# Layer 1's routing: the last three strips settled beside the first expert tiles, the first plan made later, the rows waiting on the sends themselves

## The chip, the cores and the metric

The kernel runs on one core of one Trainium2 chip. The metric is the device time of one launch in microseconds (us); the median of several runs is compared. A profiled execution has its own time, and a span from its first to its last recorded instruction.

## The reference

A two-layer "metaformer" on x of shape (2, 256, 56, 56). Each layer mixes in space (layer 0: attention in a window of 7; layer 1: two ternary 3x3 convolutions with batch norm), adds that to x, and then runs a mixture of experts over the 6272 tokens. Cut to what the change touches (layer 1's experts):

```
t = tokens of x                      # 6272 x 256
u = layer norm of t
logits = u @ gate_w + gate_b         # 8 experts
cw = the two largest of softmax(logits), zero elsewhere
out = sum over e of cw[:, e] * (gelu(u @ W1[e] + b1[e]) @ W2[e] + b2[e])   # hidden 512
t = t + out
```

All of it is float32.

## The kernel before

The experts are not run over all tokens. Each token is sent to its two experts, so that the expert matmuls run over sorted rows.

**Strips.** The tokens lie in 14 strips (7 of 8 image rows for each of two images). A strip has 3 groups of 128 tokens when its number is even and 4 when it is odd. `strip(i)` is a generator with five steps: (1) load the residual `back` (SP), add the convolution's result (DVE L2208, ACT L2211), transpose to token layout (PE `pt`, L2221); (2) add `back` (DVE L2225) and take statistics; (3) scale into `u` (ACT L762); (4) transpose `u` (PE `pu`, L810) and multiply with the gate (PE `pl`, L822); (5) write the logits `lgs` (DVE L831).

**Settling.** `settle(strips)` takes a batch of strips and gives each of their tokens its two experts and its two places in the DRAM table `xs`, which has a region for each expert. It is a generator too: best expert (DVE), second expert (DVE), ranks within the expert (PE `rk`, L892 to L895, with DVE `hots` ahead), places (DVE L904 to L908); then one step for each group, which issues two indirect DMAs from POOL (L929) that scatter the group's rows into `xs`. The batches are strips 0 to 4 one by one, then 5-6, 7-8, 9-10, 11-12 and 13.

**Early and late.** Strips 0 to 8 are early (`FIRST[1]` is 9): their 31 groups are sent while strips are worked on. After strip 8 has been settled, enough rows are known to fill 23 full tiles of 256 rows (`EARLY[1]`). `tiles(0)` plans these: a matmul counts the rows by expert (PE `counts`, L985), some 20 DVE operations find for each tile its expert and its first row (`where`). The sends of strips 9 to 13 are held back (`held`) and go out beside the tiles.

**The loop.** `all_strips()` runs 16 iterations. In iteration i, strip i does its step 1, strip i-1 its steps 2 to 4, and strip i-2 its last step; when strip i-2 ends a batch, the first three steps of its `settle` follow, and the fourth comes in the next iteration. In iteration 11, once strip 8's sends have been issued, the first plan is made and `fence()` issues a small DMA on POOL that reads `xs`. In iteration 13 `next(experts1)` has SP load the weights of tiles 0 to 2 (L1140, 1154 KB each; the expert's number is read from `where`). After the loop the second plan is begun, SP reads what the fence brought (`value_load(fences[0])`, L2328), and the expert stage starts.

**The expert stage.** SP fetches the rows `xg` of tiles 0 to 4 (L1129, 260 KB each; there are 41 full tiles and 23 half tiles in all). For each tile PE transposes the rows (`pt`, L1150), multiplies with W1 (`ph`, L1182) and W2 (`py`, L1201); ACT applies GELU, DVE adds the bias (`y`, L1211), POOL scatters the result into `ys` (L1213). Rows are fetched 4 tiles ahead and weights 3. Four times in each tile `beside1` takes a step of `rest()`: in each tile one held group is sent, and two steps are done on the plans of the remaining tiles. `rest()` is brought to its end at tile 18 at the latest, since the rows of tile 23 are fetched at tile 19.

**Order.** SP, DVE, PE and ACT take their instructions in program order (`manual_schedule(engines=ENGINES)`); POOL is not among them. The fetch of an early tile's rows is declared free of dependences on all sends (`rows1`); the fence stands in for them. PSUM: the strips use a pool of their own (`route_ps`) that is closed before the tiles' pool (`pt` 2, `ph` 4, `py` 2 banks) is opened.

The lines after the last tile gather each token's two results and write the output.

Of the kernel before, what the change touches and what calls it, by code (L numbers as in the profile page):

```python
# [2 lines left out]

# [1 line left out]

# [639 lines left out]
def metaformer(ctx: ExitStack, tc: tile.TileContext, a: dict, out: bass.AP, flag):  # L645
# [5 lines left out]
    class Banks:  # L651

        def __init__(self, pool, wide=False):
            self.pool, self.wide = pool, wide

        def tile(self, *args, **kw):
            return self.pool.tile(*args, **kw)

    def disjoint(inst, group, others):

        inst = inst.ins
        tc.declare_no_dep(inst, group=others, reason="rows apart")
        tc.add_to_no_dep_group(group, inst)
# [432 lines left out]
    def experts_in_order(layer, FF, plans, ys, wp, at_tile):  # L1096
# [25 lines left out]
        def fetch_rows(j):  # L1122
            where, _, _, n = planned(j)
            r = nc.sync.value_load(
                where[0:1, 1, n : n + 1], min_val=0, max_val=E * ROWS - G
            )
            gp = blocks_of(j)
            xg = tp.tile([P, GP, RW], F32, tag="xg", name="xg", bufs=6)
            o = nc.sync.dma_start(  # L1129
                xg[:, :gp], xs[bass.ds(r, gp * P), :].rearrange("(p i) c -> p i c", i=gp)  # L1130
            )
            if tiles[j][0] == 0:
                disjoint(o, f"early{layer}", f"rows{layer}" if layer else f"late{layer}")
            live.setdefault(j, {})["xg"] = xg

        def fetch_weights(j):
# [702 lines left out]
    with mid:  # L1839
# [338 lines left out]
        with ExitStack() as both:  # L2178
            wp1 = both.enter_context(
                tc.tile_pool(name="moe_w1", bufs=4, side="right", reuse_waits="tile")  # L2180
            )
            wp = both.enter_context(
                tc.tile_pool(name="route_w1", bufs=1, side="right", reuse_waits="tile")
            )
            tp = both.enter_context(
                tc.tile_pool(name="route_t1", bufs=2, side="right", reuse_waits="tile")
            )
            route_ps = ExitStack()
            ps = Banks(
                route_ps.enter_context(  # L2190
                    tc.tile_pool(name="route_ps1", bufs=2, space=PSUM, reuse_waits="tile")
                ),
                True,
            )

            nr = wp.tile([P, KC, RING], F32, tag="nr", name="nr")

            def residual(i):

                b, s = STRIPS[i]  # L2200
                r = X[b, s]
                ng = groups_of(i)[1]
                cols = ring(i)
                back = tp.tile([P, NTT, C], F32, tag="back", name="back", bufs=1)[:, :ng]
                nc.sync.dma_start(back, by_token(x_mid, i))
                for o in range(KC):
                    ro = r[:, o, :].rearrange("p (h w) -> p h w", w=W)
                    nc.vector.scalar_tensor_tensor(  # L2208
                        ro, ro, scale2[:, o : o + 1], inner(b, s)[:, :, o], ALU.mult, ALU.add
                    )  # L2210
                    nc.scalar.activation(  # L2211
                        in_blocks(nr[:, o, cols]),
                        narrow(ro),
                        AF.Relu,
                        bias=shift2[:, o : o + 1],
                    )
                pt = ps.tile([P, NTT, C], F32, tag="pt", name="pt")[:, :ng]
                for t in range(ng):
                    at = in_ring(i, t)
                    for k in range(KC):  # L2220
                        nc.tensor.transpose(  # L2221
                            pt[:, t, k * P : (k + 1) * P], nr[:, k, at], ident
                        )
                yield
                nc.vector.tensor_tensor(XT[b, s], pt, back, ALU.add)  # L2225

            def strip(i):
                yield from residual(i)
                yield from norm(i, XT[STRIPS[i]])

            norm, settle, tiles, planning, gates, wgt1, _, sent = routing(1, wp, tp, ps)

            def fence():

                some = wp.tile([1, 1], I32, tag="some", name="some")
                nc.gpsimd.dma_start(some, xs[0:1, 0:1].bitcast(I32))
                fences.append(some)

            def send(steps, i):

                if i >= FIRST[1]:
                    if next(steps, steps) is not steps:
                        held.append(steps)
                else:
                    finish(steps)

            def all_strips():

                n = len(STRIPS)
                jobs = {}  # L2250
                ready = iter(())
                for i in range(n + 2):
                    young, old = i - 1, i - 2
                    if young in jobs:
                        next(jobs[young])
                    send(ready, old - 1)
                    if not plans1 and FIRST[1] - 1 in sent:
                        plan, n_early = tiles(0)
                        plans1.append(plan)
                        fence()  # L2260
                    if young == 0:
                        next(jobs[young])
                    if i < n:
                        jobs[i] = strip(i)
                        next(jobs[i])
                        if i == n - 1:

                            next(experts1)
                    if young > 0 and young in jobs:
                        next(jobs[young])  # L2270
                    steps = iter(())
                    if old in jobs:
                        finish(jobs.pop(old))
                        for q in BATCHES:
                            if q[-1] == old:
                                steps = settle(q)
                    for _ in range(3):
                        next(steps, None)
                    if old == 0:
                        finish(steps)  # L2280
                    if young in jobs:
                        next(jobs[young])
                    ready = steps
                send(ready, n - 1)
                return n_early

            def last_plans():

                plan, n_full = yield from planning(1, n_early, True)
                plans1.append(plan)  # L2290
                yield
                plans1.append((yield from planning(2, n_full, True)))

            def rest():

                yield
                sending = chain(*held)
                while True:
                    more = next(sending, sending) is not sending
                    yield  # L2300
                    for _ in range(2):
                        more |= next(planned, planned) is not planned
                        yield
                    if not more:
                        return
                    yield

            plans1, fences, held = [], [], []
            gating = gates()

            def beside1(j, part):
                nonlocal route
                if route is None:
                    if part == 3:
                        next(gating, None)
                    return
                more = next(route, route) is not route
                if not more or part == 3 and j == EARLY[1] - ROWS_AHEAD - 1:
                    finish(route)
                    route = None  # L2320

            experts1 = experts_in_order(1, 2 * C, plans1, ys[1], wp1, beside1)
            route = rest()
            with tc.manual_schedule(engines=ENGINES):
                n_early = all_strips()
                planned = last_plans()
                next(planned)
                nc.sync.value_load(fences[0])  # L2328

                route_ps.close()  # L2330
                for b in range(B):
                    pads[b].close()
                tp1 = both.enter_context(tc.tile_pool(name="moe_t1", bufs=2, reuse_waits="tile"))
                ps1 = Banks(
                    both.enter_context(
                        tc.tile_pool(name="moe_ps1", bufs=2, space=PSUM, reuse_waits="tile")
                    ),
                    True,
                )
                experts1.send((tp1, ps1))  # L2340

    with ExitStack() as st:
# [164 lines left out]
```

## Time and profile before

| | us |
|---|---|
| median of 5 runs | 1715.0 (1711.0 to 1722.8) |
| profiled execution, its own time | 1719.84 |
| its span | 1718.0 |
| layer 1's routing, about 1125 to 1263 | 138 |
| expert tiles, about 1263 to 1645 | 382 |
| gathering and output, from about 1645 | 73 |

Over the span, PE is busy 1502.1 us (87%), DVE 960.1 (56%), ACT 694.6 (40%) and POOL 636.2 (37%). Times in the views are from the span's start. PE is TensorE's matmuls, PEld its weight loads, SPq the DMA issues of SP. In a line of the timeline stand the start, the duration, engine, line and operation, the tile written and those read, the shapes, the count, and in brackets how long the engine had been idle and what ended that. The matmuls' ends are modelled, and a releaser is inferred.

### The profile page before, as it was taken

Reading aid. Unit: us, or ns where it says so; the run is one execution under the profiler, and the core shown is the slowest. Engines: PE = TensorE matmul, PEld = TensorE weight load, DVE = VectorE, ACT = ScalarE, POOL = GpSimd, SP = SyncE. Lnnn points to the kernel's source line nnn. Section 1 sums busy time; section 2 is a strip of 40 time slices with the busy share of each in tenths; the row PEclk is TensorE's granted clock in tenths of the full one; section 3 lists DMA queues with packets and bytes.
Section 4 is the critical chain, followed back from the end, with each engine's and each line's share of the span. In section 5 each row is a group of like instructions: output and inputs, shape, how many; then the busy total and the mean of one; then the engine's idle time right before and its main releaser. Section 6 shows DMA issues by size and latency. Waiting matters only on the chain. (4 is left out here: it accounts for less than half of the span.)

```text
span 1718.0 us, 25578 instructions
## 1 busy us (share of the span) xinstructions
PE 1502.1 (87%) x8445; PEld 1176.8 (69%) x8445; DVE 960.1 (56%) x2620; ACT 694.6 (40%) x1419; POOL 636.2 (37%) x729
## 2 busy tenths in 40 slices
PE   5999999999878979894989879957679999999964
PEld 3556565556566867783778778746578888898852
DVE  3456667466645445976998888677743111111136
ACT  2545443453433434543444262244433334343323
POOL 2112335244343773551333323427725542222210
PEclk9999999899888999996999989955579999999975
DMA  7123334121256877984431000024457777888858
GB/s 231 56 64 91 109 98 154 34 88 62 75 170 238 286 255 292 310 302 182 173 144 71 1 1 0 10 65 143 156 186 268 272 258 266 284 288 295 297 195 322
DMA packets 94189, 291.78 MB, mean 170 GB/s; under 512 B 20183, under 2 KB 35643, under 8 KB 84960
## 3 DMA queue, kind: packets, MB, share of 16 engines
q1 hardware_dynamic: 70384, 231.82, 40.5%
q0 software_dynamic: 19856, 51.82, 7.9%
q10 hardware_dynamic: 3808, 6.42, 1.0%
q8 instruction: 69, 1.13, 0.3%
q14 instruction: 72, 0.59, 0.1%
HBM read 218.55 MB, written 74.20 MB: 170 GB/s over the span
## 5 line engine op out<-in xcount | busy, mean ns | idle before, releaser
L1182 PE MATMUL ph<-ut,w 128*128 128x256 f32 (+1 forms) x1472 | 309.5, 361 | 12.7 <-DMA w<-in_L_experts 10.8
L1211 DVE TENSOR_TENSOR y<-py,w 128x512 f32<-128x512 f32 (+1 forms) x120 | 76.8, 640 | 407.0 <-PE py L1201 387.3
L1201 PE MATMUL py<-w,h 128*128 128x256 f32 x1288 | 299.2, 381 | 2.2 <-DVE y L1211 2.2
L1182 PEld LDWEIGHTS ph<-ut,w 128*128 128x128 f32 x1472 | 250.9, 195 | 41.5 <-DMA w<-in_L_experts 12.3
L1201 PEld LDWEIGHTS py<-w,h 128*128 128x128 f32 x1288 | 244.7, 191 | 35.5 <-DVE y L1211 2.6
L929 POOL DMA_INDIRECT xs<-u,pos x196 | 194.7, 993 | 112.8 <-issue 36.3
L1213 POOL DMA_INDIRECT ys<-y,dest x136 | 136.2, 1002 | 218.0 <-DVE dest L1157 95.5
L1189 ACT ACTIVATE h<-ph,w 128x256 f32<-128x256 f32 (+1 forms) x368 | 162.8, 448 | 111.5 <-PE ph L1182 105.9
L1592 ACT ACTIVATE ex<-sc 112x476 f32<-112x476 f32 (+3 forms) x224 | 116.8, 573 | 178.0 <-PE sc L1582 176.7
L1154 ACT COPY ut<-pt 128x512 f32<-128x512 f32 (+1 forms) x120 | 65.2, 543 | 272.4 <-PE pt L1150 272.3
L1923 PE MATMUL pc<-lo,wq 128*128 128x448 f32 x336 | 133.8, 400 | 5.7 <-DVE lo L1898 5.4
L1923 PE MATMUL pc<-hi,wq 128*128 128x448 f32 x336 | 132.5, 396 | 2.4 <-DVE x L1945 1.9
L1612 DVE TENSOR_TENSOR acc<-av,acc 128x238 f32<-128x238 f32 (+3 forms) x224 | 88.3, 407 | 72.8 <-PE av L1602 72.0
L1213 POOL DMA_INDIRECT ys<-y,to x81 | 81.7, 1009 | 121.8 <-DVE dest L1157 63.5
L1602 PE MATMUL av<-ex,vals 112*64 112x238 f32 (+3 forms) x896 | 123.8, 399 | 2.8 <-DVE acc L1612 2.8
L2066 PE MATMUL pc<-hi,wq 128*128 128x448 f32 (+1 forms) x288 | 102.9, 367 | 17.8 <-ACT hi L2033 9.4
L1573 PE MATMUL sc<-q_im,keys 32*112 32x238 f32 (+3 forms) x896 | 100.3, 428 | 7.5 <-ACT ex L1592 7.4
L2066 PE MATMUL pc<-lo,wq 128*128 128x448 f32 (+1 forms) x288 | 102.1, 364 | 0.2 <-DVE lo L2034 0.2
L1896 POOL TENSOR_TENSOR v<-pad 128x928 f32<-128x928 f32 (+1 forms) x28 | 56.9, 2042 | 105.0 <-ACT pad L1879 61.0
L1602 PEld LDWEIGHTS av<-ex,vals 112*64 112x64 f32 x896 | 56.5, 141 | 51.8 <-issue 28.3
L1150 PE MATMUL pt<-ident,xg 128*128 128x128 f32 x434 | 70.3, 283 | 17.4 <-DMA xg<-xs 13.7
L1573 PEld LDWEIGHTS sc<-q_im,keys 32*112 32x112 f32 x896 | 46.3, 176 | 48.8 <-ACT ex L1592 24.1
(279 smaller groups left out, 2484.6 us busy)
## 6 DMA issues: line engine op xcount, KB each, us to landing
w<-in_L_experts SPq DMA_DIRECT2D x64, 1154.0 KB
w<-in_L_experts SPq DMA_DIRECT2D x56, 641.0 KB
xg<-xs SPq DMA_DIRECT2D x97, 260.0 KB
acc<-in_fresh SPq DMA_DIRECT2D x14, 896.0 KB
got<-ys SPq DMA_DIRECT2D x21, 512.0 KB
got<-ys SPq DMA_DIRECT2D x7, 1024.0 KB
xt<-in_x_tok SPq DMA_DIRECT2D x14, 448.0 KB
rec<-shares SPq DMA_DIRECT2D x28, 224.0 KB
```

Of the source, the lines that this page charges most:

```text
L929: w = nc.gpsimd.indirect_dma_start(xs[:, :], bass.IndirectOffsetOnAxis(ap=pos[:, j, t0 + t : t0 + t + 1], axis=0), at_of[t][0][:, at_of[t] ...
L1182: nc.tensor.matmul(ph[:, :g], w1[:, k, f * P : (f + 1) * P], d["ut"][:, k, :g], start=k == 0, stop=k == KC - 1,)
L1189: nc.scalar.activation(d["h"][:, f, :g], ph[:, :g], AF.Gelu, bias=b1[:, f : f + 1])
L1201: nc.tensor.matmul(py[:, i, :], d["h"][:, f, i * P : (i + 1) * P], w2[:, f, :], start=f == 0, stop=f == NF - 1,)
L1211: nc.vector.tensor_tensor(y[:, :gp], py[:, :gp], bcast(b2, 1, [P, gp, C]), ALU.add)
L1213: o = nc.gpsimd.indirect_dma_start(ys[:, :], bass.IndirectOffsetOnAxis(ap=d["to"][:, i : i + 1], axis=0), y[:, i, :], None, bounds_check=T ...
L1573: nc.tensor.matmul(sc[h // 2][:, h % 2, :nq], keys[g][p, c, tx * TT : (tx + 1) * TT], q_im[p, c, r0:r1, c0:c1], start=True, stop=False,)
L1592: nc.scalar.activation(e[:, :, :nq], sc[j][:, :, :nq], AF.Exp, scale=HD**-0.5)
L1602: nc.tensor.matmul(av[VW * i : VW * (i + 1), :nq], vals[g % 3][:, tx, 2 * c + j, 2 * i : 2 * i + 2, :].rearrange("p a d -> p (a d)"), ex[j ...
L1612: added = nc.vector.tensor_tensor(d, av[:, :nq].rearrange("p (h w) -> p h w", w=c1 - c0), d, ALU.add)
L1923: nc.tensor.matmul(pc[:, :NT], wq[:, k, c, dx * C + o * P : dx * C + (o + 1) * P], part[:, :, k, dx : dx + W], start=m == 0, stop=m == 2 * ...
L2066: nc.tensor.matmul(pc[:, : 2 * ns * W], wq[:, k, c, dx * C + o * P : dx * C + (o + 1) * P], part[:, : 2 * ns, k, dx : dx + W], start=m == ...
```

## The change

1. The first plan `tiles(0)` and `next(experts1)` (the weights of tiles 0 to 2) move from iterations 11 and 13 to iteration 14. Strip 13's fourth step (`pu`, `pl`) is moved ahead of them in that iteration.
2. The last two batches (strips 11-12 and 13) are no longer settled in the loop. `settling()` does their four steps beside the tiles, ahead of the later plans; `sends()` takes up their sends when it gets to them.
3. The fence is gone. The fetch of an early tile's rows is declared free of the held sends alone (`late1`), and so waits for the early sends themselves.
4. The strips' PSUM pool is closed by the time the moved steps run, so `Banks` has a lender: their tiles (`rk`, `counts`) are then taken from the rotation of `py`.

```
     class Banks:
         def __init__(self, pool, wide=False):
-            self.pool, self.wide = pool, wide
-
-        def tile(self, *args, **kw):
-            return self.pool.tile(*args, **kw)
+            self.pool, self.wide, self.lender = pool, wide, None
+
+        def tile(self, shape, dt, **kw):
+            if self.lender is None:
+                return self.pool.tile(shape, dt, **kw)
+            t = self.lender.tile([P, G // P, C], dt, tag="py", name=kw["name"])
+            t = t.rearrange("p a b -> p (a b)")[: shape[0], : int(np.prod(shape[1:]))]
+            if len(shape) == 3:
+                t = t.rearrange("p (a b) -> p a b", b=shape[2])
+            return t
...
             if tiles[j][0] == 0:
-                disjoint(o, f"early{layer}", f"rows{layer}" if layer else f"late{layer}")
+                disjoint(o, f"early{layer}", f"late{layer}")
...
-            def fence():
-
-                some = wp.tile([1, 1], I32, tag="some", name="some")
-                nc.gpsimd.dma_start(some, xs[0:1, 0:1].bitcast(I32))
-                fences.append(some)
...
                     send(ready, old - 1)
-                    if not plans1 and FIRST[1] - 1 in sent:
-                        plan, n_early = tiles(0)
-                        plans1.append(plan)
-                        fence()
                     if young == 0:
                         next(jobs[young])
                     if i < n:
                         jobs[i] = strip(i)
                         next(jobs[i])
-                        if i == n - 1:
-
-                            next(experts1)
                     if young > 0 and young in jobs:
+                        next(jobs[young])
+                    if i == n:
                         next(jobs[young])
                     steps = iter(())
                     if old in jobs:
                         finish(jobs.pop(old))
-                        for q in BATCHES:
+                        for q in BATCHES[:-2]:
                             if q[-1] == old:
                                 steps = settle(q)
+                    if i == n:
+                        plan, n_early = tiles(0)
+                        plans1.append(plan)
+                        next(experts1)
                     for _ in range(3):
                         next(steps, None)
                     if old == 0:
                         finish(steps)
-                    if young in jobs:
+                    if young in jobs and i < n:
                         next(jobs[young])
                     ready = steps
...
+            def settling():
+
+                for q in BATCHES[-2:]:
+                    steps = settle(q)
+                    for _ in range(4):
+                        next(steps)
+                        yield
+                    held.append(steps)
+                yield from last_plans()
+
+            def sends():
+
+                at = 0
+                while at < len(held):
+                    yield from held[at]
+                    at += 1
...
-                sending = chain(*held)
+                sending, others = sends(), settling()
                 while True:
                     more = next(sending, sending) is not sending
                     yield
                     for _ in range(2):
-                        more |= next(planned, planned) is not planned
+                        more |= next(others, others) is not others
                         yield
...
                 n_early = all_strips()
-                planned = last_plans()
-                next(planned)
-                nc.sync.value_load(fences[0])
-
                 route_ps.close()
...
+                ps.lender = ps1
                 experts1.send((tp1, ps1))
```

More of the change, by code (lines that the diff above doesn't have):

```diff
@@ L1 @@
 from contextlib import ExitStack, nullcontext
-from itertools import chain
 import numpy as np
@@ L2306, in rest @@
                     yield
-            plans1, fences, held = [], [], []
+            plans1, held = [], []
             gating = gates()
```

## Prediction

> **What bounds the kernel now.** I read the slices of the page first, to find the stage of the change; then the busy time by stage; then the timeline of that stage, the chain of waits in it, the waits of SP's queue, and the DMA traffic in short windows.
>
> The busy time by stage (us, then busy us and count of PE, PEld, DVE, ACT, POOL, then granted clock, DMA share, GB/s):
>
> ```profile
> 1125.00:1263.00 138.00, 90.69 (x452) 77.44 (x452) 100.81 (x420) 60.52 (x119) 74.63 (x154) 0.56 0.43 143
> 1263.00:1645.00 382.00, 381.40 (x2036) 339.69 (x2037) 68.77 (x255) 144.96 (x321) 134.18 (x136) 0.99 0.77 267
> ```
>
> The first row is the routing of layer 1's 14 strips: no engine is full, PE is at half clock, and the end is set by a chain that hops between DVE, PE and ACT. The second row is the 64 expert tiles: PE is busy 381.4 of 382 us, so a tile stage that starts x us later ends x us later, and PE work put into it is paid in full. The change touches only the seam. The timeline there:
>
> ```profile
> 1219.84 0.17 PE L985 MATMUL counts<-seen_b,all_w 128*128 128x8 bf16 x1
> 1220.06 0.17 DVE L987 COPY counts<-counts 128x8 f32<-128x8 f32 x1 [2.95 <-PE counts L985]
> ...
> 1223.88 0.17 DVE L1054 CAST where<-first 1x23 int32<-1x23 f32 x1
> ...
> 1226.14 2.35 PE L2221 MATMUL pt<-ident,nr 128*128 128x128 f32 x8 [6.13 <-ACT nr L2211]
> ...
> 1239.34 2.97 SPq L1140 DMA_DIRECT2D w<-in_L_experts  x3
> ...
> 1240.43 0.96 POOL L929 DMA_INDIRECT xs<-u,pos  x1 [0.30 <-issue]
> ...
> 1249.19 0.61 POOL L2236 DMA_DIRECT2D some<-xs  x1 [7.80 <-DMA xs<-u,pos]
> ...
> 1254.79 4.78 SPq L1129 DMA_DIRECT2D xg<-xs  x5
> ...
> 1255.97 3.16 PE L822 MATMUL pl<-gate,ut 128*128 128x8 f32 x14 [0.26 <-ACT ut L813]
> ...
> 1259.16 0.19 DVE L831 TENSOR_TENSOR lgs<-pl,gate_b 128x32 f32<-128x32 f32 x1 [4.81 <-PE pl L822]
> ...
> 1263.36 1.95 PE L1150 MATMUL pt<-ident,xg 128*128 128x128 f32 x8
> ```
>
> To be seen: the first plan (counts to where) holds DVE up in mid strips, and PE then sits idle 6.13 us ahead of strip 11's transposes. The weights of tiles 0 to 2 leave SP at 1239.34 and drain beside the last strips. The fence lets the rows go at 1254.79, and PE ends the gate products (pl) of strip 13 at 1259.13. The last settle runs on DVE from 1259.16, and PE, which takes its instructions in order, starts tile 0 (pt, L1150) at 1263.36. Weights and rows are there by then: what ends last is the settle.
>
> **The change part by part**, against this execution (span 1718.0, its own time 1719.84 us; the median of the five runs is 1715.0, 4.8 lower, and I move the sum over to it unchanged).
>
> *The first plan leaves iteration 11.* Strips 7 to 9 are 16.70 us apart (transposes at 1185.97 and 1202.67), 9 to 11 are 23.47. The excess, 6.8, and the idle time on PE, 6.1, bound the gain; I take 6.5. The chain of waits puts POOL's sends in here, since DVE's write into u (L803) follows a landing; but that gap is 0.17 to 0.27 us with a landing ahead of it and without one, and the buffer belongs to strip 3, whose sends were issued by 1188.42. So I don't let the sends bind.
>
> *The settle of strips 11 and 12 leaves the strips.* Strip 13's scaling ended at 1251.61, its transposes (L810) began at 1253.35, behind the settle's matmuls: 1.5 us less. Together PE ends pl of strip 13 at 1259.1 - 6.5 - 1.5 = 1251.1.
>
> *The plan is made in iteration 14, behind that.* In program order the counts matmul stands after pl of strip 13. Counts to the end of the second cast took 1219.84 to 1224.05, 4.2 us: 1255.3. SP loads the expert's number and issues: 1238.6 to 1239.34, 0.75 us. So the weights start at 1256.1, where before they started at 1239.34, 24 us ahead of the first tile. Queued behind that wait on SP are two more weights (1.32 apart) and the rows of tiles 0 to 4, the first at 1259.8. Nobody else waits for SP there.
>
> *Weights and rows through the DMA queue.* This is the term that decides. Three weights are 3 x 1154 KB = 3.55 MB. Alone on the queue they moved 0.85 MB in 2 us, at the slowest 0.68:
>
> ```profile
> DMA packets 103, 0.85 MB, mean 425 GB/s; under 512 B 11, under 2 KB 11, under 8 KB 11
> ...
> DMA packets 75, 0.68 MB, mean 338 GB/s; under 512 B 1, under 2 KB 1, under 8 KB 2
> DMA packets 177, 0.60 MB, mean 299 GB/s; under 512 B 27, under 2 KB 27, under 8 KB 137
> ```
>
> (windows 1248:1250, 1262:1264, 1264:1266.) So 8.4 to 10.5 us, after about 0.95 from issue to first traffic (rows issued at 1254.79, traffic from 1255.75): the third weight is in at 1265.4 to 1267.5. The last two windows say where rows issued behind a weight stand: the rows of tile 5 went out at 1261.47, 1.1 us after a weight, and while that weight drained (1262 to 1264) only 2 of 75 packets were small; the rows' small packets came after it. So tile 0's 260 KB follow all three weights: 0.6 us at 425 GB/s, 1.2 at the 218 of window 1258:1260, and 0.3 to land. pt of tile 0 starts at 1266.3 to 1269.0; I take 1267.4, or 4.0 us later than 1263.36.
>
> The Trainium skill says the same in general and thereby speaks against this change (DMA: Bandwidth & Descriptors, section "Queues, rings and completion order"): each DMA engine consumes one issuer's ring in order and round-robins only between issuers. The rows share SP's ring with the weights.
>
> *Work put into the tiles.* The matmuls of two settles (0.31 us from 1236.86 to 1237.17, about 0.3 for strip 13) and the second counts (0.19) now stand between products: +0.8 on a full PE. Waits there I cost at nothing. A step's DVE operations take about 1.3 us and PE reaches the matmul a half tile and more later (half a tile is 3.5 us); uncovered, 1.3 for each of three. A borrowed py buffer makes the next py wait for the y add just before (0.69 us), under 3.46 us of ph; uncovered, 0.9 each. DVE is busy 69 of 382 us there. The 18 held groups of sends still leave POOL one per tile (to tile 17); the later plans, 2 steps per tile, end near tile 12 instead of 8, ahead of their use at tile 19, so seven tiles of 7.35 us cover them.
>
> *The clock.* PE is now idle some 16 us before tile 0 instead of 4. Before, the clock was full 3.8 us after pt began (0.50 to 1267, 0.87 in 1267:1268). At layer 0's first tile, after a longer idle time, PE began at about 496.7 and stood at 0.50 until 502 and 0.83 in 502:504, some 5.9 us. Two us more at half clock lose 1: 0 to 1.1, I take 0.5. The Trainium skill (TensorE: Matmul & The Clock Gate, Part 1) has one idle window of about 3.4 us make PE cold, so that both waits would be equally cold; by it this term would be 0 and the sum 4.8.
>
> *The fence goes.* Costed at nothing: before, xg(0) was in hand before PE needed it, and afterwards the last early send (issued by 1241.4, 2.5 to 4.3 us to land) is in 14 us before the rows can be issued at 1259.8. The send is not what the rows hang on; the plan and SP's queue are.
>
> Sum: 4.0 + 0.8 + 0.5 = +5.3 us: 1725.1 in this execution, 1720.3 on the median. That is 0.3%; 0.5% (8.6 us) is about what a measurement of this kernel can tell from no change. The ends: +2.9 + 0.6 + 0 and +5.6 + 0.9 + 1.1, so 1718.5 to 1722.6 for this case alone, and some 3 us either way for the medians (the runs lie from 1711.0 to 1722.8).
>
> **The rivals.**
> 1. Rows do not queue behind weights. Then xg(0) lands 2.7 us after its issue, 1262.5, with the first weight (about 5 us after 1256.1, by the one issued at 1260.34) already in; tile 0 starts 0.9 earlier, and 1.3 is given back: 1715.4. Against it stand the two windows above. Chance 0.07, no change.
> 2. Slower by over 0.5%: the weights take as long as they did. From 1239.34 it was 1254 until the queue had emptied (5 packets of it still ran in 1252:1254), 14.6 us, beside 0.5 MB of other loads and some sends. Were that the weights' own pace, a few slow DMA engines for instance, xg(0) would be in at 1256.1 + 14.6 + 1.2 = 1271.9: +8.5 + 1.3, or 1724.8. It decides once pt of tile 0 starts after 1270.7 (1263.4 + 8.6 - 1.3). If the sends do bind the strips after all, the 6.5 is lost and the place is the same: 1726.8. Only 3.3 us of rows in the queue separate it from the forecast, so: chance 0.36 with both.
> 3. The parts pay: plan and settle off the strips' path are worth 8.0, the last settle's idle time 4.2. To be faster by 8.6, tile 0 must start by 1253.5, before the plan itself (1255.3) can be had. It would take counts that don't stand behind pl of strip 13: about 1705. Chance 0.07.
>
> **How the numbers follow.** The forecast has 0.50 and rival 1 0.07, together 0.57 within 0.5%; slower 0.36, faster 0.07. The range reaches down past rival 1 by 3 us of the medians, to 1712, and up past rival 2 by as much, to 1730.
>
> **What would show it.** Right: strip 11's transposes follow pl of strip 9 without the 6 us; pl of strip 13 ends near 1251; weights leave SP near 1256; SP no longer waits for sends; PE's longest idle time is about 16 us and ends with a DMA (xg), near 1267; then 7.35 us per tile as before. Wrong: rows landing before the third weight, pt of tile 0 before 1263 or after 1271, or PE waits inside tiles 1 to 5.

## The result, and the profile after

The kernel after takes 1722.0 us, the kernel before 1717.3 in the same comparison (medians of 52 and 94 runs); the ratio is 1.0027, with a 95% interval of 1.0019 to 1.0036, or 3.3 to 6.2 us slower (0.27%). The forecast was +5.3 us, and no change beyond 0.5%. The profiled execution has a span of 1719.4 us and a time of its own of 1721.13.

The two profiled executions reach the strips at different times, for reasons that lie ahead of the change: the first residual transposes (`pt<-ident,nr`) start at 1125.99 us before and at 1124.11 after. The last product of the tiles ends 4.7 us later from that start; the spans differ by 1.4 us only because 1.9 us ahead of the strips and 1.5 us behind the tiles, where nothing was changed, went the other way. So in what follows places are given from that start ("S+"), and lines as the profile has them.

The busy time by stage (us, then busy us and count of PE, PEld, DVE, ACT, POOL, then granted clock, DMA share, GB/s):

```profile
1125.00:1263.00 138.00, 89.70 (x438) 76.32 (x436) 93.09 (x378) 59.24 (x117) 74.18 (x153) 0.56 0.38 130
1263.00:1645.00 382.00, 379.46 (x2036) 337.50 (x2037) 75.25 (x293) 144.83 (x321) 133.79 (x136) 0.99 0.79 271
```

DVE has handed 6 to 8 us of settling from the first stage to the second, where it is idle most of the time. The timeline of the seam:

```profile
1217.99 1.95 PE L2226 MATMUL pt<-ident,nr 128*128 128x128 f32 x8
...
1238.81 0.96 POOL L934 DMA_INDIRECT xs<-u,pos  x1 [0.30 <-issue]
...
1241.08 2.07 ACT L767 ACTIVATE u<-x,t_nmr,t_rstd 128x256 f32<-128x256 f32 x4 [0.49 <-DMA xs<-u,pos]
1241.27 0.17 DVE L808 COPY u<-ids 128x4 f32<-128x4 f32 x1 [0.27 <-DMA xs<-u,pos]
...
1241.74 2.80 PE L815 MATMUL pu<-ident,u 128*128 128x128 f32 x8 [1.50 <-ACT u L767]
...
1245.21 3.16 PE L827 MATMUL pl<-gate,ut 128*128 128x8 f32 x14 [0.26 <-ACT ut L818]
...
1248.22 0.17 PE L990 MATMUL counts<-seen_b,all_w 128*128 128x8 bf16 x1
1248.44 0.17 DVE L992 COPY counts<-counts 128x8 f32<-128x8 f32 x1 [6.92 <-PE counts L990]
...
1252.25 0.17 DVE L1059 CAST where<-first 1x23 int32<-1x23 f32 x1
...
1252.81 2.94 SPq L1145 DMA_DIRECT2D w<-in_L_experts  x3
...
1256.67 4.79 SPq L1134 DMA_DIRECT2D xg<-xs  x5
...
1264.77 1.97 PE L1155 MATMUL pt<-ident,xg 128*128 128x128 f32 x8 [16.38 <-DMA xg<-xs]
```

Strip 11's transposes (first line) no longer wait. The gate products of strip 13 (L827) end near 1248.4, S+124.3, where before it was S+133.1. And then PE stands idle for 16.38 us, released by a DMA, the rows of tile 0. They are the last to come, behind plan, three weights and SP's queue. What SP waited for in that stretch (us in total, times, longest):

```profile
SPq L1143 <- DVE first L1058: 22.1, 1, 22.1
```

That is the load of tile 0's expert number, which waits for the plan. There is no row for the sends: when the rows were issued, the last early send had landed 15 us before (at 1241.25 by its semaphore, 2.4 us after its issue at 1238.81).

The order of weights and rows on the DMA engines can be read from the packets in windows of 2 us (1256:1258, 1260:1262, 1262:1264 and 1264:1266; weights have packets of 9232 bytes, rows of 2080):

```profile
DMA packets 103, 0.80 MB, mean 402 GB/s; under 512 B 16, under 2 KB 16, under 8 KB 16
...
DMA packets 101, 0.80 MB, mean 402 GB/s; under 512 B 14, under 2 KB 14, under 8 KB 14
...
DMA packets 221, 0.77 MB, mean 386 GB/s; under 512 B 25, under 2 KB 25, under 8 KB 170
...
DMA packets 437, 0.81 MB, mean 405 GB/s; under 512 B 48, under 2 KB 48, under 8 KB 437
```

Rows were issued from 1256.67 on, but up to 1262 the windows have not one packet between 2 and 8 KB: only the weights' large ones and tiny ones. From 1264 on no large packet is left. The three weights were in at 1264.0, 11.2 us after the first was issued, and tile 0's rows 0.7 us after that.

### The profile page after: what moved, and what is told of

The parts are those of the page before. It is cut to its first block, busy times and chain, and to the rows that moved or that the text cites. A ratio compares the mean times of both kernels' runs of the same rounds, so it can differ in the third digit from the quotient of the medians.

```text
span 1719.4 us, 25573 instructions
## 1 busy us (share of the span) xinstructions
PE 1502.4 (87%) x8445; PEld 1175.8 (68%) x8445; DVE 958.8 (56%) x2620; ACT 693.9 (40%) x1419; POOL 636.1 (37%) x728
## 5 line engine op out<-in xcount | busy, mean ns | idle before, releaser
L1607 PE MATMUL av<-ex,vals 112*64 112x238 f32 (+3 forms) x896 | 125.3, 403 | 3.3 <-DVE acc L1617 3.3
L1218 POOL DMA_INDIRECT ys<-y,to x81 | 81.6, 1008 | 124.3 <-DVE dest L1162 63.5
L1155 PEld LDWEIGHTS pt<-ident,xg 128*128 128x128 f32 x434 | 55.8, 146 | 48.1 <-DMA xg<-xs 24.5
```

The lines of the kernel that those rows point to most:

```text
L1155: nc.tensor.transpose(pt[:, k, i * P : (i + 1) * P], d["xg"][:, i, k * P : (k + 1) * P], ident)
L1218: o = nc.gpsimd.indirect_dma_start(ys[:, :], bass.IndirectOffsetOnAxis(ap=d["to"][:, i : i + 1], axis=0), y[:, i, :], None, bounds_check=T ...
L1607: nc.tensor.matmul(av[VW * i : VW * (i + 1), :nq], vals[g % 3][:, tx, 2 * c + j, 2 * i : 2 * i + 2, :].rearrange("p a d -> p (a d)"), ex[j ...
```

## The experiments

The eight kernels below the kernel after were each timed against the kernel before on the same chip, in five rounds. The places below are from each one's trace, in us from the start of the strips' first transposes; "tile 8" is the first W2 product of the ninth tile, a point at which the seam and the first settles are over.

| kernel | plan ready | first weight out | first rows out | strip 13's pl ends | tile 0 starts | tile 8 | ratio to before (95%) |
|---|---|---|---|---|---|---|---|
| before | 98.1 | 113.3 | 128.8 | 133.1 | 137.4 | 206.4 | 1 |
| after | 128.3 | 128.7 | 132.6 | 124.3 | 140.7 | 210.4 | 1.0027 (1.0019 to 1.0036) |
| later_plan_alone | 131.5 | 131.9 | 135.8 | 127.5 | 144.2 | 213.3 | 1.0037 (1.0012 to 1.0062) |
| no_fence | 98.1 | 113.8 | 121.9 | 133.4 | 137.7 | 206.6 | 0.9997 (0.9981 to 1.0012) |
| plan_where_it_was | 98.1 | 113.8 | 122.9 | 131.1 | 131.0 | 200.2 | 0.9975 (0.9959 to 0.9992) |
| rows_first | 128.3 | 128.7 | 130.0 | 124.3 | 135.1 | 205.9 | 0.9995 (0.9976 to 1.0014) |
| plan_ahead | 121.3 | 121.7 | 125.5 | 124.2 | 134.0 | 203.7 | 0.9986 (0.9965 to 1.0007) |
| plan_ahead_rows_first | 121.3 | 121.7 | 122.9 | 124.2 | 128.6 | 199.3 | 0.9935 (0.9913 to 0.9957) |
| plan_in_steps | 111.0 | 111.4 | 121.4 | 125.0 | 125.3 | 195.9 | 0.9950 (0.9924 to 0.9975) |
| plan_in_steps_rows_first | 111.3 | 111.7 | 119.4 | 125.4 | 125.2 | 195.7 | 0.9941 (0.9916 to 0.9966) |

The times agree with the places, with one exception: divided by 1717, the shift at tile 8 is +0.23% for the kernel after, -0.36% for plan_where_it_was and -0.62% for the last, inside their intervals, as are all others but plan_ahead_rows_first. That one is 7.1 us (0.42%) earlier at tile 8, while its interval begins at 0.43% and its middle is 0.65%; where the other 4 us would come from no run shows. Matmul ends are modelled, so tile 0 can "start" 0.15 us ahead of pl's end.

**The parts by themselves.** First the later plan without the rest, in the kernel before:

```
-                    if not plans1 and FIRST[1] - 1 in sent:
-                        plan, n_early = tiles(0)
-                        plans1.append(plan)
-                        fence()
...
-                        if i == n - 1:
-
-                            next(experts1)
...
                     if young in jobs:
                         next(jobs[young])
+                    if i == n:
+                        plan, n_early = tiles(0)
+                        plans1.append(plan)
+                        fence()
+                        next(experts1)
                     ready = steps
```

> The kernel before, with one edit: the first plan, the fence and the three weights are made in iteration 14, behind the gate products of strip 13; all settles stay in the strips. Theory A (the late plan is the loss): the strips gain the 6.5 us of the plan, but the weights leave SP near 131 us after the strips' first transposes (before: 113.3), the rows land behind them near 143, and tile 0 starts 5 to 6 us later than in the kernel before (137.4); the time is 5 to 6 us above the kernel before, a little more than in the kernel after, which also has the settles out of the way (1.5 us). Rival D (moved settles and py buffers are the loss): with the settles left in place the time is at or below the kernel before.

Measured: weights out at S+131.9, tile 0 at S+144.2, 6.9 us later than before; the time 0.37% up. Theory A holds, and the loss is about 1 us more than it expected (5 to 6 us): the strips gained 5.7 us in place of 6.5. PE's timeline shows both waits that follow one another there:

```profile
1269.10 0.18 PE L892 MATMUL rk<-hots,before_w 128*128 128x32 bf16 x1 [8.29 <-DVE hots L882]
...
1277.57 1.97 PE L1150 MATMUL pt<-ident,xg 128*128 128x128 f32 x8 [7.10 <-DMA xg<-xs]
```

The settle of strip 13 still stands in the strips, but it is over 7 us before the rows are in. Set against the kernel after, which differs from it in the moved settles and the fence, the settles are worth 2.9 us at tile 8 (213.3 to 210.4): they are a gain. (That the fence is worth nothing is the next run.)

Then the fence alone, in the kernel before:

```
-                disjoint(o, f"early{layer}", f"rows{layer}" if layer else f"late{layer}")
+                disjoint(o, f"early{layer}", f"late{layer}")
...
-                        fence()
...
-                nc.sync.value_load(fences[0])
```

> The kernel before, with one edit: the fence and its load are gone, and the rows of early tiles wait on the early sends themselves, as in the kernel after. Theory A (the fence was hidden, the last settle ends last): rows leave SP some 5 us earlier (the last send lands near 1249, the fence at 1254), tile 0 starts at the same place behind the settle, no change in time (within 1 us). Rival: the fence was on the path, and the time falls by 3 us or more, or the wait on many sends costs SP time, and it rises.

Measured: rows out 6.9 us earlier, tile 0 no earlier, time unchanged. The fence was hidden behind the last settle; in the timeline PE still waits for that (`hots`) and not for rows:

```profile
1267.67 0.21 PE L892 MATMUL rk<-hots,before_w 128*128 128x32 bf16 x1 [2.98 <-DVE hots L882]
...
1268.93 1.95 PE L1150 MATMUL pt<-ident,xg 128*128 128x128 f32 x8
```

Then all of the change but the later plan:

```
                     send(ready, old - 1)
+                    if not plans1 and FIRST[1] - 1 in sent:
+                        plan, n_early = tiles(0)
+                        plans1.append(plan)
...
                         next(jobs[i])
+                        if i == n - 1:
+                            next(experts1)
...
-                    if i == n:
-                        plan, n_early = tiles(0)
-                        plans1.append(plan)
-                        next(experts1)
```

> The kernel after, with the plan put back to iteration 11 and the weights back to iteration 13, as in the kernel before; the settles stay beside the tiles and the rows wait on the early sends. Theory A (the loss is the late plan alone, the moved settles are a gain): strips end some 6.5 us later than in the kernel after, but weights are in long before, so tile 0 follows the gate products of strip 13 within 1 us: about 6 us earlier than in the kernel before, less 0.6 given back in the tiles, so 5 us below the kernel before (0.3%). Rival D (the moved settles cost): tile 0 starts earlier and the time is still not below the kernel before. Rival B (the wait on the sends costs more than the fence): the rows leave SP later than 1254.8 on the clock of the kernel before, PE is idle for over 4 us, and nothing is won.

Measured: tile 0 follows strip 13 without a gap, 6.4 us earlier than before, and the time is 0.25% down:

```profile
1253.96 3.16 PE L827 MATMUL pl<-gate,ut 128*128 128x8 f32 x14 [0.26 <-ACT ut L818]
1256.98 1.95 PE L1155 MATMUL pt<-ident,xg 128*128 128x128 f32 x8
```

So the moved settles and the wait on the sends, which the change has in common with this kernel, are good for 6.2 us at tile 8 when the weights are early; in the kernel after, the later plan turns them into +4.0. Here the rows do hang on the last early send, as SP's waits show:

```profile
SPq L1134 <- DMA xs<-u,pos: 5.2, 1, 5.2
```

**The path of the kernel after.** Two edits cut it at two places. One lets rows out ahead of the second and third weight:

```
         for j in range(AHEAD):
             live[j] = {}
-            fetch_weights(j)
+            if not layer or j == 0:
+                fetch_weights(j)
         tp, ps = yield
         for j in range(ROWS_AHEAD):
             fetch_rows(j)
+            if layer and 0 < j < AHEAD:
+                fetch_weights(j)
```

> The kernel after, with one edit: in layer 1 SP issues the weights of tile 0, then the rows of tiles 0 and 1, then the weights of tile 1, rows 2, weights 2, rows 3 (before: three weights, then the rows). Theory A (the rows queue behind three weights in SP's ring): with the plan where it is, tile 0's rows follow one weight instead of three; that weight landed 5 us after its issue, so tile 0 starts some 6 us earlier than in the kernel after (16.4 us of idle time on PE become about 10), and the time falls by about 6: some 1.5 us below the kernel before. Rival B (the rows are held by the wait on the early sends, or DMA engines do not keep the order): the start of tile 0 moves by less than 1.5 us and the time stays about 4.7 above the kernel before. Rival C (the weights themselves are the wait, the rows would be in anyway): tile 0 starts earlier but tile 1 then waits for its weights, and the gain is below 3 us.

Measured: the plan and the first weight go out as in the kernel after; the rows go out only 2.6 us earlier, but tile 0 starts 5.6 us earlier, and the time falls from 1.0027 to 0.9995. The rows were held by the two weights ahead of them: 2.6 us in SP's issues, the other 3.0 us on the DMA engines. Rival B falls with that, and rival C too: PE has no other wait in the first tiles, and at tile 8 the gain is still 4.5 us (the last section says where 1.1 us went).

```profile
1262.00 2.24 PE L1155 MATMUL pt<-ident,xg 128*128 128x128 f32 x8 [10.78 <-DMA xg<-xs]
```

The other makes the plan while PE is at strip 13's gate products:

```
-                    if i == n:
-                        next(jobs[young])
                     steps = iter(())
...
                         next(experts1)
+                        next(jobs[young])
```

> The kernel after, with one edit: in iteration 14 the first plan and the three weights stand ahead of strip 13's fourth step (pu, pl) instead of behind it. DVE is idle there for 6.9 us in the kernel after. Theory A (the late plan delays weights, and rows stand behind them): the plan runs beside pu and pl, the weights leave SP 6 to 7 us earlier, tile 0 starts 6 to 7 us earlier, and the time is about 2 us below the kernel before. Rival B (the early sends hold the rows): the last of them lands near 1241 in the kernel after, so B expects no move unless that landing is later than the plan; the time stays 4.7 above. Rival D (the settle steps and the borrowed py buffers beside the tiles cost the time): the start of tile 0 moves, but at least 4 us are still lost inside tiles 0 to 5.

Measured: plan, weights and tile 0 all 6.7 to 7.0 us earlier, strip 13 no later: DVE had been idle. At tile 8 it is 2.7 us below the kernel before; the timed ratio, 0.9986, has 1 in its interval and agrees.

```profile
1263.82 1.97 PE L1155 MATMUL pt<-ident,xg 128*128 128x128 f32 x8 [9.79 <-DMA xg<-xs]
```

**Versions that beat both.** The two edits together:

> The kernel after, with both edits: the plan stands ahead of strip 13's fourth step, and SP issues weights 0, rows 0 and 1, weights 1, rows 2, weights 2, rows 3. Theory A: the two delays add up, since each is a part of the same path (plan, weights, rows): the weights leave near 121.7 us after the strips' first transposes, tile 0 starts 6.4 us after that, near 128, 9 us earlier than in the kernel before (137.4), of which about 2 are given back within the first tiles (0.6 for the settles, 1 for tile 1's weights); the time is 7 us (0.4%) below the kernel before. Rival: the edits overlap, and the time is not below that of the better one alone (2 to 3 us below the kernel before).

Measured: tile 0 at S+128.6, tile 8 at 7.1 us below the kernel before, ratio 0.9935. Tile 0 is 12.1 us earlier than in the kernel after, against 5.6 and 6.7 for the two edits alone. They add up, so plan, weights and rows are indeed one path. PE still waits 4 us for it. So the plan was spread over the places where DVE waits for PE, and the weights were put back to iteration 13:

```
                     young, old = i - 1, i - 2
+                    if i == FIRST[1] + 3:
+                        for _ in range(4):
+                            next(early)
...
                     steps = iter(())
+                    if i == FIRST[1] + 2:
+                        next(early)
+                    if i == n - 1:
+                        plan, n_early = finish(early)
+                        plans1.append(plan)
+                        next(experts1)
                     if old in jobs:
...
-                    if i == n:
-                        plan, n_early = tiles(0)
-                        plans1.append(plan)
-                        next(experts1)
                     for _ in range(3):
                         next(steps, None)
+                    if i == FIRST[1] + 1:
+                        early = planning(0)
+                        next(early)
```

> The kernel after, with the first plan taken in steps in the places where DVE waits for PE (its counts in iteration 10 behind the settle of strips 7 and 8, the rest in iterations 11, 12 and 13), and the weights in iteration 13 again. Theory A: the plan costs the strips at most 2 us instead of 6.5, weights are in before the strips end, the rows leave when the last early send has landed (near 122, beside the weights), and tile 0 starts near 126, 11 us earlier than in the kernel before: the time is 10 us (0.6%) below it. Rival (DVE has no room in the strips, so that the plan costs its 4.7 us wherever it stands): the strips end near 129 and the gain is that of the plan put back to iteration 11, about 5 us.

Measured: the plan costs the strips 0.8 us (S+124.3 to 125.0) in place of 6.5, tile 0 waits 0.3 us for its rows, and tile 8 is 10.5 us below the kernel before; timed 0.9950:

```profile
1248.84 3.16 PE L827 MATMUL pl<-gate,ut 128*128 128x8 f32 x14 [0.26 <-ACT ut L818]
1252.30 1.97 PE L1155 MATMUL pt<-ident,xg 128*128 128x128 f32 x8 [0.29 <-DMA xg<-xs]
```

Last, the same with rows first:

> As plan_in_steps, and SP issues the weights of tile 0, then rows 0 and 1, weights 1, rows 2, weights 2, rows 3. Theory A: with one weight instead of three beside the last early sends, these land near 117 to 119 instead of 122.5, rows are in before PE has ended the gate products of strip 13, and tile 0 starts with their end, near 124.5 to 125.5: 0 to 1.5 us less than plan_in_steps. Rival: the weights of tiles 1 and 2, now issued behind the rows, which wait for the sends, come too late for those tiles, and the time is above that of plan_in_steps.

Measured: the rows go out at S+119.4 instead of 121.4, since only one weight drains beside the last sends, but tile 0 can't start before strip 13 has ended: 125.2, no more than 0.2 us gained at tile 8, nor do the later weights come too late. Ratio 0.9941; the two can't be told apart. With either, PE goes from the strips to the tiles with next to no gap (0.3 us and none), so what is left to win ahead of tile 0 lies in the strips themselves.

## Why the prediction was right, point by point

*What bounds.* Right: the end of the seam is set by what PE waits for last, once the settle and now the rows, and a later tile stage costs its delay in full: +3.3 us at tile 0, +4.0 at tile 8, +4.0 at tile 19, +4.7 at the last product. The last 0.7 us come after tile 23, far behind the seam; about half of them are short waits of PE for a weight there (0.6 us in the kernel after, 0.3 before), which differ from trace to trace.

*The strips.* 8.0 us were expected, 8.9 came. The plan's removal gave 6.3 to 6.6 (strip 11's transposes at S+93.9 for 100.1, strip 13's at S+111.2 for 117.7), as sized. The settle of strips 11 and 12 gave 2.3 where I had 1.5: I let PE start strip 13's transposes after the whole scaling, but in the kernel after they start 0.66 us after it begins (L815 at 1241.74, scaling from 1241.08) and follow it group by group. The sends did not bind the strips: where the view names one (1241.27), the gap is 0.27 us, and it was 0.27 at the same place in the kernel before (1249.73), where no landing ended it.

*Plan and SP.* 4.20 us from counts to the second cast, as before. From there to the issue it was 0.39 us instead of 0.75, where SP had been standing at the load.

*Weights and rows.* The term that decided: 11.3 us expected from the first weight's issue to tile 0, 12.0 measured (0.7 more). The order was the forecast's, and rows_first shows it to be the cause. In the Trainium skill (DMA: Bandwidth & Descriptors, "Queues, rings and completion order") descriptors are consumed in ring order on each engine; the windows above and the 5.6 us of rows_first agree. Rival 1 is out with that. Rival 2 is out too: with nothing else beside them the weights took 11.2 us, not 14.6, and the third landed within 0.8 us on all engines.

*Work in the tiles.* +0.8 expected; from tile 0 to tile 8 it is 0.7 longer, and PE has no wait for `hots`, nor for a py buffer, in the first tiles. The later plans and sends cost nothing that shows there.

*The clock.* +0.5 expected, 0.1 measured: after 16.4 us of idle time the full clock came 4.1 us after PE began, before it was 3.9. The rule of the Trainium skill (TensorE: Matmul & The Clock Gate, Part 1), that one idle window makes PE cold, so that a longer wait makes it no colder, gave 0 and was nearer than the row of layer 0 that I took; the granted clock was 0.50 ahead of tile 0 in both profiles. The row of layer 0 (5.9 us) was not about the longer wait: the last section has 6.2 us after a shorter one.

*The fence.* Nothing, as costed: no_fence. The rival on the other side that I called a gain (counts not behind pl of strip 13) was not in the change, but plan_ahead shows that it can be done. By itself it is not worth the ten us of that rival: plan_ahead is 2.7 us below the kernel before at tile 8, and only with the plan taken in steps is it 10.5.

The sum was 5.3; its terms as measured are 3.3 + 0.6 + 0.1 = 4.0 in the two profiled executions, and the timed difference of 3.3 to 6.2 us holds both. That the sum came so close is in part luck: the strips gave 0.9 us more than forecast and SP took 0.4 less, while weights and rows took 0.7 more, and these misses nearly cancel. What moved in opposite directions (8.9 won on the strips, 12.2 lost to plan, weights and rows) left so little that 0.5% was not reached.

## What to carry to other kernels

In this kernel a transfer was due when what stood ahead of it in its queue had drained, not when it was issued (the rows of tile 0 landed 8.1 us after their issue behind three weights, 2.7 us after it in the kernel before, where the weights were in): before moving an issue, write down what it will stand behind, and let what is needed first go out first (one weight, its rows, then the rest). Work that decides on transfers (here a plan that only needs early counts) belongs where its engine waits anyway, taken in steps, well ahead of the transfers' use. And when several parts go in together, run them one by one: here a good part, the settles, worth 6 us, was covered up by the later plan, which alone costs 7, and the fence was worth nothing.

## What the runs showed of the hardware

Small sends beside bulk loads landed much later: the last early send landed 2.4 us after its issue in the kernel after, where only sends were on the DMA engines, and 7.4 and 8.4 us after it in no_fence and plan_where_it_was, with three weights draining beside it (S+114.4 to 121.7 and 122.8). In plan_in_steps_rows_first, with one weight, it took 4.5 us.

The time that PE takes to get to the full clock did not follow how long it had been idle: 3.9 us after 9.8 us of idle time (plan_ahead), 4.1 after 16.4 (after), 6.2 after 10.8 (rows_first), and 5.7 in plan_in_steps, where it had hardly been idle at all (0.3 us) but had run at 0.50 during the strips. It is read from the granted clock of short windows, the first number behind the busy times; here the kernel after, from 1264.77, and rows_first, from 1262.00:

```profile
1268.00:1269.00 1.00, 1.00 (x4) 0.81 (x3) 0.00 (x0) 0.99 (x2) 0.69 (x2) 0.57 0.95 401
```

```profile
1267.00:1268.00 1.00, 1.00 (x4) 0.80 (x3) 0.89 (x6) 0.31 (x1) 0.37 (x1) 0.50 0.99 415
1268.00:1269.00 1.00, 1.00 (x6) 0.89 (x5) 0.24 (x3) 0.28 (x2) 0.69 (x2) 0.91 0.89 352
```

The 2.1 us between these two are about 1.1 us of the tile stage at half clock, and that is why rows_first lost 1.1 of its 5.6 us between tile 0 and tile 8. A likely cause stands in the traces' records of the clock: in each trace all its changes lie on a grid of 3.41 us (the full-clock stretch of the tiles is 389.12 us, 114 steps, in six traces and 392.53 us, 115 steps, in four), and the ten times from tile 0 to the full clock, 3.1 to 6.2 us, differ by less than one step. So it would be where on that grid tile 0 begins; that was not tried.
